# Softmax probabilities turned by VectorE and a way through DRAM instead of TensorE turns

## The chip, the cores and the metric

The kernel runs on one core of a Trainium2 chip. The metric is the device time of one execution in microseconds (us): the median of three runs. The core has five engines with queues of their own. TensorE (PE) multiplies matrices, VectorE (DVE) and GpSimd (POOL) do elementwise work and reductions, ScalarE (ACT) does exponentials and copies, and SyncE (SP) issues transfers. Sixteen DMA engines move data between on-chip memory (SBUF) and DRAM. Matmuls write to PSUM, eight banks of on-chip memory.

## The reference, cut to what matters

A two-layer decoder works on 16 blocks of 128 tokens with 512 features. Six parts follow each other, each added to x and normalized:

```python
x = _layernorm(x + _L0_attn_ref(x, ...))            # stage 1: softmax attention, 16 heads of 32, 4 key heads
x = _layernorm(x + _L0_xattn_ref(x, ctx_512, ...))  # stage 2: latent attention, 16 heads, keys = values = ctx rows
x = _layernorm(x + _L0_ffn_ref(x, ...))             # stage 3: ternary FFN
x = _layernorm(x + _L1_attn_ref(x, ...))            # stage 4: linear attention with decay
x = _layernorm(x + _L1_xattn_ref(x, ctx_512, ...))  # stage 5: causal softmax attention, 16 heads of 32
x = _layernorm(x + _L1_ffn_ref(x, ...))             # stage 6: mixture of experts
```

The softmax attentions, stages 1, 2 and 5, all have this form, for each block and head:

```python
scores = q @ k.T            # 128 queries x 128 keys
p = softmax(scores + mask)
out = p @ v                 # then projected and added to x
```

TensorE sums over the partitions (rows) of its operands. The softmax leaves p with the queries on the partitions; the product with the values needs the keys there. So each 128 x 128 square of p has to be turned.

## The kernel before

All of x stays in SBUF. Each stage is written as Python loops that a planner unrolls: it places each instruction in its engine's queue by the times of its own model, so the order on an engine is mostly not the order of the source. `tc.keep_in_program_order` pins an instruction behind the one traced before it on the same engine. On the chip each engine's queue then runs strictly in that order, SP's too.

Stages 1 and 5 share `attend`. Step n of its loop writes the scores of block n into four PSUM banks (`score`, L446 in stage 1 and L939 in stage 5). It then goes through four parts c. In each part the class `Softmax` starts one quarter of the block's heads (mask sum L184 and maximum L186 on VectorE, four exponentials L191 on ScalarE), finishes an earlier quarter (reciprocal L197 on VectorE, product L198 on POOL), and turns a quarter of block n - 1 (`turn`: four transposes L203 on TensorE into a PSUM bank, one copy L205 back by VectorE). At the top of the step the values of block n - 2 are multiplied (`value`, L452 and L946), copied by ScalarE (L246), and in part 1 projected, added to x and normalized (`project_out`, L148, L149, L110 to L121). The other parts are filled by `Share.deal` with tasks that prepare the next group of four blocks: transposes of x, projections, and in stage 1 the folding of stage 2's weights (`folds`), whose 1.7 MB pieces SP loads into two buffers (L391). In stage 5's last group there are no tasks left; in stage 1's last group only folds.

Stage 2 works in 32 steps: four groups, two halves of eight heads, four blocks each. Step m computes scores (`Heads`, L576), the softmax, and in `turn` lets VectorE transpose p in squares of 32 x 32 (L590) without moving the squares between rows. Four heads go through one such instruction. The values (L600) make up for that: sixteen products, each with 32 rows of keys and 256 columns, four in different row quarters of the array, with a copy of the keys (`rep`) in the matching order. The `rep` copies are loaded from a DRAM buffer, `dkv`, to which the rotated context is written first (L383, L538). Step m's order in the source is: scores and softmax of m, first half of the projection of m - 2 (`out(0)`, L613), values of m - 1, second half of the projection of m - 2 (`out(1)`), then `pieces`, which loads two 352 KB pieces of FFN weights on SP (L466) and reduces or cuts earlier ones on VectorE.

Stage 5's start also fills 20 MB of DRAM with zeros for stage 6 (L899), and stage 6's copies of x to DRAM (`sums<-x`, L987) are issued by SP while stage 5 still runs.

Of the kernel before, what the change touches and what calls it, by code (L numbers as in the profile page):

```python
# [12 lines left out]
F32 = mybir.dt.float32  # L13
# [5 lines left out]
P = 128  # L19
NB = 16  # L20
D = 512
# [24 lines left out]
def decoder_kernel(ctx: ExitStack, tc: tile.TileContext, a: dict, out: bass.AP):  # L46
# [22 lines left out]

    psum = Banks()  # L70
# [4 lines left out]
    psum.share(mm=2, sc=4, pt=2)  # L75
# [98 lines left out]
    class Softmax:  # L174
# [5 lines left out]
        def start(self):  # L180
            src = self.sc
            if self.mask is not None:
                src = self.pool.tile([P, 4, P], F32, tag="t", name="t", bufs=3)
                nc.vector.tensor_tensor(src, self.sc, bc(self.mask, 4), ALU.add)  # L184
# [3 lines left out]
            if self.p is None:  # L188
                self.p = self.pool.tile([P, 4, P], F32, tag="p", name="p", bufs=5)
# [10 lines left out]
        def turn(self):  # L200
            pt = bank("pt", [P, 4, P], "pt")
            for j in range(4):
                nc.tensor.transpose(pt[:, j, :], self.p[:, j, :], ident)  # L203
            self.pT = self.pool.tile([P, 4, P], F32, tag="pT", name="pT", bufs=4)
            nc.vector.tensor_copy(self.pT, pt)  # L205
# [21 lines left out]
    def attend(pool, mask, wo, prepare, score, value):  # L227


        held = {}  # L230
# [3 lines left out]
        for n in range(NB + 2):  # L234
# [7 lines left out]
            if n >= 2:  # L242
                av = bank("pt", [P, KC, P], "av")
                value(av, n - 2, [s.pT for s in held.pop(n - 2)])
                oT = pool.tile([P, KC, P], F32, tag="oT", name="oT")
                nc.scalar.copy(oT, av)  # L246
            for c in range(4):
# [5 lines left out]
                if 1 <= n <= NB:  # L253
                    held[n - 1][c].turn()
                if c == 1 and n >= 2:
                    project_out(oT, wo, n - 2)
                else:
                    share.deal()
# [52 lines left out]
    with tc.tile_pool(name="p1", bufs=1) as p1:  # L311
# [52 lines left out]
        dkv = dram.tile([NB, P, DC], F32, tag="dkv", name="dkv")  # L364
# [8 lines left out]
        def rotate(g, ct, kvr, t2):  # L373
# [4 lines left out]
            def turn():  # L378
# [4 lines left out]
                nc.sync.dma_start(dkv[blocks].rearrange("b l d -> l b d"), kvr)  # L383
# [64 lines left out]
        def value(av, n, pT):  # L448
            v = groups[n // GB][1]
            for c in range(KV):  # L450
                rows = slice(c * HD, (c + 1) * HD)
                nc.tensor.matmul(av[rows], lhsT=v[:, n % GB, rows], rhs=pT[c], start=True, stop=True)  # L452
# [52 lines left out]
    with tc.tile_pool(name="p2", bufs=1, reuse_waits="tile") as p2:  # L505
        psum.share(mm=2, sc=2, av=4)
# [19 lines left out]

        Q = P // 4
# [3 lines left out]
        def context(g, kvr):  # L533
            reps = []
            for i in range(GB):
                rep = p2.tile([P, 4, DC], F32, tag="rep", name="rep", bufs=GB + 1)
                for qi in range(4):
                    nc.sync.dma_start(  # L538
                        rep[qi * Q : (qi + 1) * Q], dkv[g * GB + i].rearrange("(kj k) d -> k kj d", k=Q)
                    )  # L540
                reps.append(rep)
# [8 lines left out]
            return xT, kvT, reps  # L550
# [17 lines left out]
        class Heads:  # L568
            def __init__(self, b, half, qT, kT, rep):
                self.b, self.half, self.rep = b, half, rep  # L570
# [9 lines left out]
                self.turned = p2.tile([P, 8, 4, Q], F32, tag="pT", name="pT", bufs=2)  # L580
# [5 lines left out]
            def turn(self):  # L586
                p = self.p
                for par, s in enumerate(self.soft):
                    s.finish()
                    nc.vector.transpose(  # L590
                        self.turned[:, 4 * par : 4 * par + 4].rearrange("p h k q -> p (h k q)"),
                        p[:, par].rearrange("p h k -> p (h k)"),
                    )

            def values(self):
                av = [bank("av", [P, 8, Q], "av") for _ in range(4)]
                for kj in range(4):
                    for qi in range(4):
                        rows = slice(qi * Q, (qi + 1) * Q)
                        nc.tensor.matmul(  # L600
                            av[qi], lhsT=self.rep[rows, kj, :], rhs=self.turned[rows, :, kj, :],
# [826 lines left out]
```

## Time and profile before

| what | value |
|---|---|
| median of 3 runs | 2106.39 us (2104.89 to 2107.31) |
| the profiled execution | 2109.23 us, span 2107.5 us |
| PE, DVE, ACT, POOL busy | 97%, 41%, 30%, 31% of the span |
| mean granted TensorE clock | 0.995 |
| stage 1, first to last scores | 34.1 to 234.3 us |
| stage 2, first scores to last values | 283.9 to about 753 us |
| stage 5, first to last scores | 1314.2 to 1497.8 us |

A row of the profile's groups reads: line, engine, operation, output<-input, shapes, count, then busy time in us and the mean length of one in ns, then the idle time of the engine just before and what ended it. A row of the timeline reads: start, length, engine, line, operation, count. Float32 matmuls appear as two instructions each. An instruction's length includes its way through the pipeline, so neighbours overlap; what one costs its engine is seen from start to start. [...]

### The profile page before, as it was taken

What the parts mean: (1) busy time and instruction counts of PE and PEld (TensorE: products, weight loads), DVE (VectorE), ACT (ScalarE), POOL (GpSimd) and SP (SyncE); (2) the same over time, 40 slices, a digit from 0 to 9 for tenths busy, and PEclk for the clock granted to TensorE, in tenths of its full rate; (3) what the DMA queues carried; (4) which work ended last, traced back from release to release, by engine and by line L of the source; (5) the groups of instructions that cost most, each with busy time, mean ns of one, the idle gap of its engine ahead of it and who ended that gap; (6) DMA issues with size and microseconds to landing.
All of it is one profiled execution on the core that took longest, in us unless ns stands there. A gap on an engine that the chain in (4) does not pass through costs nothing. (4 is left out here: it accounts for less than half of the span.)

```text
span 2107.5 us, 26857 instructions
## 1 busy us (share of the span) xinstructions
PE 2053.2 (97%) x10117; PEld 1148.5 (54%) x10117; DVE 853.9 (41%) x1728; ACT 626.0 (30%) x2167; POOL 648.2 (31%) x674
## 2 busy tenths in 40 slices
PE   8999999999999999999999999999899999999997
PEld 5555554445454458888555444555544455555552
DVE  4667733444554243222123313777731122222224
ACT  3655533323333222222211112766622200000002
POOL 5565521211122122223223113455603222222223
PEclk9999999999999999999999999999999999999999
DMA  6011320212220010001300008600004279999974
GB/s 230 1 35 45 112 79 24 62 43 74 60 66 6 1 54 2 1 1 39 115 1 1 1 6 258 232 21 21 27 25 147 93 244 284 303 294 293 289 229 166
DMA packets 105362, 209.99 MB, mean 100 GB/s; under 512 B 27280, under 2 KB 65552, under 8 KB 98576
## 3 DMA queue, kind: packets, MB, share of 16 engines
q1 hardware_dynamic: 90336, 101.40, 15.4%
q0 software_dynamic: 13792, 105.55, 15.2%
q8 instruction: 80, 1.31, 0.3%
q10 hardware_dynamic: 1104, 1.31, 0.2%
q14 instruction: 50, 0.41, 0.1%
HBM read 159.66 MB, written 48.57 MB: 99 GB/s over the span
## 5 line engine op out<-in xcount | busy, mean ns | idle before, releaser
L198 POOL TENSOR_TENSOR p<-p,rs 128x512 f32<-128x512 f32 x192 | 201.1, 1048 | 505.4 <-DVE rs L197 478.3
L613 PE MATMUL po<-mT,cc 128*128 128x512 f32 x512 | 236.0, 605 | 0.0
L191 ACT ACTIVATE p<-t,nmx 128x128 f32<-128x128 f32 x512 | 198.6, 390 | 34.5 <-POOL p L198 8.8
L613 PEld LDWEIGHTS po<-mT,cc 128*128 128x128 f32 x512 | 92.2, 189 | 107.2 <-issue 103.6
L191 ACT ACTIVATE p<-sc,nmx 128x128 f32<-128x128 f32 x256 | 90.2, 373 | 147.4 <-DVE nmx L186 142.1
L114 POOL TENSOR_SCALAR ve<-mv 128x1 f32<-128x1 f32 x80 | 18.1, 227 | 328.2 <-DVE mv L112 316.2
L559 PE MATMUL pq<-xT,wqr 128*128 128x512 f32 x256 | 117.5, 602 | 1.0 <-ACT xT L128 0.7
L1171 ACT ACTIVATE rsg<-rg 128x352 f32<-128x352 f32 x39 | 18.1, 464 | 336.0 <-PE rg L1166 336.0
L148 PE MATMUL po<-wo,oT 128*128 128x512 f32 x256 | 116.8, 599 | 0.4 <-ACT qkT L416 0.4
L1166 PE MATMUL rg<-ew,xsT 128*128 128x352 f32 x312 | 101.2, 466 | 14.5 <-DMA ew<-in_l1f_w_dram,which 12.7
L783 PE MATMUL pq<-xT,wq 128*128 128x512 f32 x256 | 110.9, 594 | 1.0 <-ACT xT L128 0.7
L1187 PE MATMUL ry<-ew,ractT 128*128 128x512 f32 (+1 forms) x234 | 106.9, 592 | 0.0
L121 POOL TENSOR_SCALAR x<-x,mv,rstd 128x512 f32<-128x512 f32 x48 | 100.6, 2097 | 4.5
L1166 PE MATMUL ru<-ew,xsT 128*128 128x352 f32 x312 | 98.7, 459 | 0.0
L191 ACT ACTIVATION_READ_ACCUMULATOR p<-t,nmx 128x1 f32 x512 | 96.4, 188 | 0.0
L706 POOL TENSOR_TENSOR hl<-ht,hh 128x512 fp32r<-128x512 f32 x44 | 60.5, 1375 | 114.8 <-ACT hh L704 114.8
L1137 POOL DMA_INDIRECT ew<-in_l1f_w_dram,which x39 | 38.1, 976 | 185.9 <-PE ry L1187 163.3
L1197 POOL DMA_INDIRECT sums<-ry,place x39 | 62.0, 1590 | 105.7 <-DMA sums<-ry,place 66.4
L205 DVE COPY pT<-pt 128x512 f32<-128x512 f32 x128 | 86.5, 678 | 18.1 <-PE pt L203 18.1
L203 PEld LDWEIGHTS pt<-ident,p 128*128 128x128 f32 x512 | 59.8, 141 | 53.8 <-issue 44.6
L1049 PE MATMUL pg<-xT,sw_gu 128*128 128x512 f32 x192 | 86.5, 593 | 0.0
L1173 DVE TENSOR_TENSOR ract<-rsg,ru 128x352 f32<-128x352 f32 x39 | 20.3, 521 | 158.5 <-issue 145.5
(231 smaller groups left out, 3715.4 us busy)
## 6 DMA issues: line engine op xcount, KB each, us to landing
piece<-in_l0f_w_dram SPq DMA_DIRECT2D x48, 352.0 KB
raw<-in_l0x_raw_dram SPq DMA_DIRECT2D x8, 1728.0 KB
slots_x<-zero SPq DMA_DIRECT2D x1, 10023.0 KB
sums<-zero SPq DMA_DIRECT2D x1, 9984.0 KB
xs<-slots_x SPq DMA_DIRECT2D x156, 64.0 KB
rep<-dkv SPq DMA_DIRECT2D x64, 64.0 KB
sums<-x SPq DMA_DIRECT2D x16, 256.0 KB
sum<-sums SPq DMA_DIRECT2D x16, 256.0 KB
```

The lines of the kernel that those rows point to most:

```text
L121: engine.tensor_scalar(x[b], x[b], mean, rstd, ALU.subtract, ALU.mult)
L148: nc.tensor.matmul(po, lhsT=oT[:, c, :], rhs=wo[:, c, :], start=(c == 0), stop=(c == KC - 1))
L191: nc.scalar.activation(self.p[:, j, :], src[:, j, :], AF.Exp, bias=nmx[:, j : j + 1], accum_out=self.sm[:, j : j + 1])
L198: nc.gpsimd.tensor_tensor(self.p, self.p, spread(rs, P), ALU.mult)
L205: nc.vector.tensor_copy(self.pT, pt)
L559: nc.tensor.matmul(pq, lhsT=wqr[:, k, cols], rhs=xT[:, k, :], start=(k == 0), stop=(k == KC - 1))
L613: nc.tensor.matmul(self.po, lhsT=self.cc[:, 4 * par + j, :], rhs=mT[h], start=(par == 0 and j == 0), stop=(par == 1 and j == 3),)
L783: nc.tensor.matmul(pq, lhsT=wq4[k // 2][:, k % 2, c * P : (c + 1) * P], rhs=xT[:, k, :], start=(k == 0), stop=(k == KC - 1))
L1049: nc.tensor.matmul(dst, lhsT=sw_gu[:, k, at : at + P], rhs=xTs[g][:, k, :], start=(k == 0), stop=(k == KC - 1),)
L1166: nc.tensor.matmul(dst, lhsT=self.xT[:, k, :], rhs=gu[:, k, off : off + FE], start=(k == 0), stop=(k == KC - 1),)
L1187: nc.tensor.matmul(po, lhsT=self.actT[:mw, m_, :], rhs=dn[:mw, m_, :], start=(m_ == 0), stop=(m_ == 2))
L1197: nc.gpsimd.indirect_dma_start(out=sums, out_offset=bass.IndirectOffsetOnAxis(ap=place, axis=0), in_=y, in_offset=None, compute_op=ALU.add,)
```

## The change

In stages 1 and 5, `Softmax.turn` goes. A class `Turn` takes its place, two parts behind the exponentials. For each quarter VectorE transposes the 32 x 32 squares of p from SBUF to SBUF. After two quarters (512 KB) SP writes them to a DRAM buffer; after four, SP reads the block back in four transfers, one for each set of 32 keys, so that each square arrives on its keys' rows. The values of block n - 2 are now taken up in part 1 of step n, one block after the last square, and the projection moves to part 2. The value products keep their number and shape, and each is pinned behind what precedes it on TensorE. The mask sum is written into p itself.

In stage 2 the squares go the same way, with one write of 512 KB and four reads of 128 KB a step. The values become two products over all 128 keys with 512 columns, in place of sixteen; `rep` and `dkv` go. The zeros for stage 6 are written in the second group of stage 3 instead of at the start of stage 5. PSUM banks are shared out anew.

```diff
-    psum.share(mm=2, sc=4, pt=2)
+    psum.share(mm=3, sc=4, pt=1)
...
-        def turn(self):
-            pt = bank("pt", [P, 4, P], "pt")
-            for j in range(4):
-                nc.tensor.transpose(pt[:, j, :], self.p[:, j, :], ident)
-            self.pT = self.pool.tile([P, 4, P], F32, tag="pT", name="pT", bufs=4)
-            nc.vector.tensor_copy(self.pT, pt)
+    class Turn:
+        def __init__(self, pool):
+            self.pool = pool
+            self.away = dram.tile([P, 4, 2, 8 * Q], F32, tag="away", name="away", bufs=2)
+
+        def squares(self, c, p):
+            if c % 2 == 0:
+                self.sq = self.pool.tile([P, 4, 8, Q], F32, tag="sq", name="sq", bufs=2)
+            at = slice(c % 2 * 4, c % 2 * 4 + 4)
+            nc.vector.transpose(
+                self.sq[:, :, at, :].rearrange("p k h q -> p h k q"), p.rearrange("p h (k a) -> p h k a", a=Q)
+            )
+            if c % 2:
+                nc.sync.dma_start(self.away[:, :, c // 2, :], self.sq.rearrange("p k h q -> p k (h q)"))
+            if c == 3:
+                self.back()
+
+        def back(self):
+            self.pT = self.pool.tile([P, 4, 16, Q], F32, tag="pT", name="pT", bufs=1)
+            rows = self.away.rearrange("(t a) k n f -> k a t (n f)", a=Q)
+            for k in range(4):
+                nc.sync.dma_start(self.pT[k * Q : (k + 1) * Q].rearrange("a t h q -> a t (h q)"), rows[k])
...
-                if 1 <= n <= NB:
-                    held[n - 1][c].turn()
                 if c == 1 and n >= 2:
+                    av = bank("pt", [P, KC, P], "av")
+                    held.pop(n - 2)
+                    value(av, n - 2, turns.pop(n - 2).pT)
+                    oT = pool.tile([P, KC, P], F32, tag="oT", name="oT")
+                    nc.scalar.copy(oT, av)
+                of, part = divmod(4 * n + c - 2, 4)
+                if 0 <= of < NB:
+                    if part == 0:
+                        turns[of] = Turn(pool)
+                    turns[of].squares(part, held[of][part].p)
+                if c == 2 and n >= 2:
                     project_out(oT, wo, n - 2)
...
-        psum.share(mm=2, sc=2, av=4)
+        psum.share(mm=2, sc=4, av=2)
...
             def turn(self):
-                p = self.p
+                sq = p2.tile([P, 4, 8, Q], F32, tag="sq", name="sq", bufs=2)
+                away = dram.tile([P, 4, 8 * Q], F32, tag="away2", name="away2", bufs=2)
+                self.pT = p2.tile([P, 4, 8, Q], F32, tag="pT", name="pT", bufs=2)
                 for par, s in enumerate(self.soft):
                     s.finish()
                     nc.vector.transpose(
-                        self.turned[:, 4 * par : 4 * par + 4].rearrange("p h k q -> p (h k q)"),
-                        p[:, par].rearrange("p h k -> p (h k)"),
+                        sq[:, :, 4 * par : 4 * par + 4, :].rearrange("p k h q -> p h k q"),
+                        self.p[:, par].rearrange("p h (k a) -> p h k a", a=Q),
                     )
+                nc.sync.dma_start(away, sq.rearrange("p k h q -> p k (h q)"))
+                rows = away.rearrange("(t a) k f -> k a t f", a=Q)
+                for k in range(4):
+                    nc.sync.dma_start(self.pT[k * Q : (k + 1) * Q].rearrange("a t h q -> a t (h q)"), rows[k])
...
-                av = [bank("av", [P, 8, Q], "av") for _ in range(4)]
-                for kj in range(4):
-                    for qi in range(4):
-                        rows = slice(qi * Q, (qi + 1) * Q)
-                        nc.tensor.matmul(
-                            av[qi], lhsT=self.rep[rows, kj, :], rhs=self.turned[rows, :, kj, :],
-                            start=(kj == 0), stop=(kj == 3),
-                        )
+                for par in range(2):
+                    av = bank("av", [P, 4, P], "av")
+                    tc.keep_in_program_order(nc.tensor.matmul(
+                        av, lhsT=self.keys,
+                        rhs=self.pT[:, :, 4 * par : 4 * par + 4, :].rearrange("p t h q -> p h t q"),
+                        start=True, stop=True,
+                    ))
+                    nc.scalar.copy(self.cc[:, 4 * par : 4 * par + 4, :], av)
```

## The prediction

> **What bounds the kernel now.** I read the page's busy table and slices first, then busy time in stretches that I chose by stage, then the order of time inside one block.
>
> ```profile
> span 2107.5 us, 26857 instructions
> PE 2053.2 (97%) x10117; PEld 1148.5 (54%) x10117; DVE 853.9 (41%) x1728; ACT 626.0 (30%) x2167; POOL 648.2 (31%) x674
> ```
>
> TensorE has no slack on average, so taking work from it should pay, unless another limit lies close behind. The stretches show where it does:
>
> ```profile
> 58.93:116.20 57.27, 56.59 (x388) 31.93 (x388) 39.88 (x82) 34.19 (x145) 33.13 (x33) 1.00 0.01 1
> 200.94:233.40 32.46, 32.21 (x258) 19.54 (x257) 28.51 (x60) 23.14 (x103) 18.24 (x18) 1.00 0.32 113
> 1336.94:1471.19 134.25, 132.92 (x1035) 75.28 (x1034) 98.12 (x199) 86.08 (x361) 69.05 (x70) 1.00 0.14 47
> 1479.20:1496.94 17.74, 16.81 (x177) 10.79 (x177) 17.32 (x38) 13.69 (x66) 13.67 (x14) 1.00 0.09 32
> ```
>
> Columns: stretch, length, busy PE, PEld, DVE, ACT, POOL, clock, DMA share, GB/s. Rows one and three are stages 1 and 5 with filler tasks: a block takes 14.2 and 13.4 us, VectorE is busy 9.8 of it: PE-bound. Row two, stage 1's last group, has 10.8 us a block and 9.5 of VectorE. Row four, stage 5's last group without filler, is VectorE's already: 17.32 of 17.74 us, two blocks, 8.9 each.
>
> **Stages 1 and 5: what goes.** 512 turns on PE and their 128 PSUM copies.
>
> ```profile
> L205 DVE COPY pT<-pt 128x512 f32<-128x512 f32 x128 | 86.5, 678 | 18.1 <-PE pt L203 18.1
> L203 PE MATMUL pt<-ident,p 128*128 128x128 f32 x512 | 79.2, 278 | 1.7 <-DVE pT L205 1.2 <-POOL p L198 0.5
> L590 DVE STREAM_TRANSPOSE pT<-p 128x512 f32<-128x512 f32 x64 | 45.5, 711 | 74.7 <-POOL p L198 74.7
> L1155 DVE STREAM_TRANSPOSE xsT<-xs 128x512 f32<-128x512 f32 x39 | 27.1, 698 | 0.0
> ...
> 1410.59 0.60 PE L203 MATMUL pt<-ident,p 128*128 128x128 f32 x4
> 1411.03 0.59 PE L137 MATMUL pq<-xT,wqo 128*128 128x512 f32 x1
> ```
>
> A turn lasts 278 ns, but four of them hold the next matmul back by 1411.03 - 1410.59 = 0.44 us: 0.11 us each. [...] I take the pitch, since it is what the following matmul sees: 16 x 0.11 = 1.75 us a block.
>
> In the filled part some 11 blocks of each stage turn before the last group: 11 x 1.75 = 19 us from each. Stage 1's last group stops at VectorE, about 9.8 instead of 10.8 us: 4 us. Stage 5's last group gains nothing.
>
> What takes their place on VectorE: the 128 copies at 678 ns become 128 square transposes, 698 to 711 ns by the two rows (L1155 is strided too): +0.03 us each, 4 us in all, hidden by 2.5 us of free VectorE in a filled block and on the path only in the last groups (0.5 us each). A strided transpose at half speed would add 0.7 x 4 = 2.8 us a block and fill VectorE; with a strided row at 698 I take nothing. The squares follow two parts behind the exponentials instead of four, so VectorE may wait for POOL when a layernorm (0.23 + 0.57 + 2.10 us) stands before the product; behind that wait stand the next mask sum and maximum. It eats VectorE's free time in filled blocks and costs up to 1 us a block in the last groups: +2 us in stage 5, in stage 1 inside the 9.8. The value products keep number and shape; their moving operand now comes in runs of 32 elements, as L600's does already (256 columns four at a time in 1.94/8 = 0.24 us, against half of 0.43 for 512): nothing. The mask sum in place saves a buffer, no time.
>
> **The way through DRAM.** A block issues on SP two writes of 512 KB and four reads of 256 KB; a stage 2 step one write of 512 KB and four reads of 128 KB. That is 192 + 160 new DMAs for 64 rep reads and 4 dkv writes removed. The nearest rows:
>
> ```profile
> 505.41 0.38 SPq L383 DMA_DIRECT2D dkv<-kvr  x1
> 506.00:506.50 0.50, 0.50 (x4) 0.20 (x4) 0.26 (x1) 0.50 (x2) 0.21 (x1) 1.00 0.28 83
> 506.50:507.00 0.50, 0.41 (x3) 0.30 (x2) 0.50 (x2) 0.14 (x1) 0.00 (x0) 1.00 1.04 291
> ...
> 488.45 1.75 SPq L538 DMA_DIRECT2D rep<-dkv  x4
> 490.00:490.50 0.50, 0.50 (x3) 0.19 (x2) 0.43 (x1) 0.00 (x0) 0.00 (x0) 1.00 0.44 129
> 490.50:491.00 0.50, 0.50 (x3) 0.26 (x2) 0.00 (x0) 0.00 (x0) 0.00 (x0) 1.00 0.56 149
> ```
>
> The write to DRAM starts 0.7 us after its issue and reaches 291 GB/s: 512 KB takes 1.8 us. The four 32-partition reads take 1.75 us to issue, begin to flow about 0.95 us after the first, and use half of the engines at 129 to 149 GB/s: about 280 at full use, so 512 KB takes 1.9 us and 1 MB 3.7. [...] Estimates: write 3.6 us, reads 4.0 in stage 2 and 5.8 in stages 1 and 5. [...]
>
> Stages 1 and 5: the values follow one whole block behind the last square, some 12.4 and 11.7 us in filled blocks: covered. The tails are not. In stage 5 the last scores start at 1496.94, the last multiplication ends at 1509.8, the last x sum starts at 1522.09. Now: square done 1510.6, + 9.4 trip, + 1.1 values, + 0.75 copy, + 3.7 projection = 1525.5: +3 us. Stage 1's tail likewise, +2, as stage 2's first projections can lie beside it. SP waits about 3.6 us in each block for a write; behind it stand raw, context, piece and sums DMAs, all issued a step or more ahead, so nothing. The reverse is worse: a raw load that waits for its fold (107 us at the longest today, harmlessly) can hold an away DMA. Between 0 and 12 us; I take +2. The 20 MB of zeros move to the FFN, where DMA stands at 0.00 to 0.01; matmuls there cannot mind (592 ns beside full DMA in stage 6, 594 without). Stage 5's start loses its collision: -1 of 1.7 us of idle PE.
>
> **Stage 2.**
>
> ```profile
> 481.59 1.16 PE L576 MATMUL sc<-kT,qT 64*128 64x128 f32 x16
> 482.68 3.70 PE L613 MATMUL po<-mT,cc 128*128 128x512 f32 x8
> 486.31 2.01 PE L600 MATMUL av<-pT,rep 32*128 32x256 f32 x32
> 488.25 3.70 PE L613 MATMUL po<-mT,cc 128*128 128x512 f32 x8
> ...
> 489.72 0.71 DVE L590 STREAM_TRANSPOSE pT<-p 128x512 f32<-128x512 f32 x1 [1.15 <-POOL p L198]
> ```
>
> Starts give 1.09 + 3.63 + 1.94 + 3.63 = 10.3 us a step. The values become 4 instructions of 0.43 us, and the change of row tiling before them (3.63 against 8 x 0.43) goes: 1.09 + 3.44 + 1.72 + 3.63 = 9.9, saving 0.41 x 32 = 13 us. The catch: transposes end 8.85 us after the step's scores, and in source order the values are due 9.9 + 4.7 = 14.6 after them. A trip of 5.7 us fits; 7.6 does not. If PE takes the second half of the projection (3.4 us, ready) before the values, 9.2 us fit. Only the values are pinned behind what precedes them, nothing behind them, and today's order already breaks L600 up by readiness. I count on that order, with +3 us of remaining stalls. Each half's first step has the 17 us projection as cover.
>
> **Sum.** -19 - 19 - 4 + 2 (tail) + 2 + 3 - 1 + 2 - 13 + 3 = -44 us. The profiled execution took 2109.2 us (span 2107.5): 2065; the median of the three runs is 2106.4, so 2062.
>
> That the change does not do what it says needs no rival: the turns are gone from the source, and only their order is open. **Rivals.** (a) Slower: stage 2's trip is not covered. In source order the step becomes 8.85 + trip - 4.7 us; 24 steps stand without a projection. The other terms bring -34, so it decides from 10.3 + 34/24 = 11.7 us a step, a trip of 7.6. [...] For: my estimate is on the edge. Against: the free order. (b) VectorE becomes the limit in filled blocks too, by waits for POOL or slow strided transposes: 0.7 us a block left of 1.75, -44 + 22 = 2084. Against: 2.5 us of free VectorE, L1155. (c) The order stays partly bad, or away DMAs stand behind waiting loads: 0.75 us on each of 56 value waits (16 + 24 + 16), -44 + 42: no difference, 2104. (d) The turns are worth their union of 79 us: 2045.
>
> **Chances.** Forecast 0.52, (d) 0.10, (b) 0.12, (c) 0.08, (a) 0.18. Three runs differ by 0.1%, so about 0.2% (4 us) can be told from no change. Faster 0.74, same 0.06, slower 0.20. Range 2036 to 2116: below, (d) with no tails (2045 - 9); above, (b), (c) and the edge of (a), whose rest is left out.
>
> **What would show it.** Right: L203 and L205 gone; about 12.4 and 11.7 us between score groups of filled blocks, stage 5's last group still about 9; stage 2 steps of 9.9; PE waits on the pT reads only in tails. Wrong: PE idle before stage 2's values for a DMA on each step; square transposes over 1 us; SP waits on L391 before away.

## The result, and the profile after

The changed kernel takes 2184.2 us (median of 4 runs, 2180.8 to 2184.8), the kernel before 2106.9 us: a ratio of 1.037 (95% interval 1.035 to 1.039). It is slower by 77 us, where 44 us less were forecast.

The page of the changed kernel says first that TensorE is as busy as before (2052.3 us for 2053.2), with 1408 instructions fewer:

```profile
span 2178.7 us, 24328 instructions
PE 2052.3 (94%) x8709; PEld 1122.9 (52%) x8709; DVE 852.0 (39%) x1728; ACT 623.7 (29%) x2103; POOL 647.4 (30%) x674
```

Busy time in stretches shows why. These are four blocks of stage 1's filled part, two of its last group, four filled blocks of stage 5 and five in its last group and tail (columns: stretch, length, busy PE, PEld, DVE, ACT, POOL, clock, DMA share, GB/s):

```profile
102.90:160.80 57.90, 54.15 (x319) 29.87 (x319) 38.06 (x80) 34.33 (x147) 32.44 (x32) 1.00 0.65 177
214.70:260.50 45.80, 28.15 (x130) 16.91 (x129) 20.68 (x47) 18.64 (x85) 17.79 (x18) 0.71 0.68 204
1396.80:1465.70 68.90, 61.96 (x353) 34.48 (x352) 39.28 (x80) 33.79 (x144) 27.88 (x28) 0.82 0.50 138
1538.00:1593.00 55.00, 36.25 (x241) 18.52 (x240) 27.97 (x59) 19.82 (x91) 25.37 (x25) 0.81 0.70 187
```

A filled block of stage 1 takes 14.5 us (14.3 before) and one of stage 5 17.2 (13.4 before), with idle TensorE that was not there. In the last groups TensorE is idle for more than a third of the time, the others about half of it or more. The granted clock is at 0.71 and 0.81 there, and at 0.82 in the filled blocks of stage 5, where it was 1.00. The slow clock stretches what work is left, by 47 us more than before (table below), which is why the busy time did not fall.

By stage, in the profiled runs: stage 1 (first scores to stage 2's first) 249.8 to 282.1 us, stage 2 (to the first product of stage 3) 484.7 to 483.7, stage 5 (first scores to the end of the last projection) 207.8 to 254.1. For stages 1 and 5 I add up, over windows of 2 us, TensorE's idle time and the busy time lost to the clock (busy x (1 - granted clock)). What remains of the length is work at full clock:

| kernel | stages 1 + 5 | idle | lost to the clock | work |
|---|---|---|---|---|
| before | 457.6 | 10.8 | 3.4 | 443.4 |
| changed | 536.2 | 77.9 | 50.6 | 407.7 |
| e2 without the trip | 457.8 | 43.9 | 17.3 | 396.6 |
| e7 without the trip, reordered | 439.8 | 33.2 | 19.1 | 387.5 |
| e8 rearranged, whole trip | 503.4 | 67.8 | 28.2 | 407.4 |
| e17 turns only left out | 431.9 | 21.3 | 12.6 | 398.0 |

TensorE did lose 36 us of work; 67 us of pauses and 47 us of slower clock came in its place. The waits on TensorE of the changed kernel (for what, us in all, times, longest):

```profile
PE po L149 <- ACT oT L273: 32.1, 30, 2.7
PE av L474 <- DMA pT<-away: 12.5, 2, 9.8
PE av L965 <- DMA pT<-away: 11.4, 3, 5.4
...
PE sc L958 <- DVE p L187: 9.5, 10, 3.7
PE sc L468 <- DVE p L187: 8.5, 5, 2.7
```

Only 24 us of these are waits for the trip's data. The rest are the projection behind ScalarE's copy of the values, and scores for banks that VectorE's mask sum has not yet freed. The first belongs to the copy's new place: of the kernels below it is 25.5 us in e2, and 3.3 in e6, where the copy is back in its old one. The second shows wherever the turns are gone, in e17 too, where nothing took their place (9.8 us ahead of scores, 0.5 before). One place on TensorE's timeline shows how a pause is paid twice:

```profile
1392.30 4.53 PE L958 MATMUL sc<-kT,qT 32*128 32x128 f32 x24 [3.71 <-DVE p L187]
1396.76 1.94 PE L965 MATMUL av<-pT,v 128*32 128x128 f32 x32
1399.40 6.50 PE L149 MATMUL po<-wqo,oT 128*128 128x512 f32 x8 [0.70 <-ACT oT L273]
...
1414.70 5.40 PE L149 MATMUL po<-wqo,oT 128*128 128x512 f32 x8 [2.69 <-ACT oT L273]
```

After 3.71 us of waiting, the same eight projection instructions that take 3.6 us elsewhere take 6.50: from 1391.4 to 1405.1 the granted clock is 0.50.

SP's queue in stage 1's last group shows what the trip's reads stand behind:

```profile
219.61 0.31 SPq L225 DMA_DIRECT2D pT<-away  x1
224.89 0.36 SPq L413 DMA_DIRECT2D raw<-in_l0x_raw_dram  x1
225.29 1.76 SPq L225 DMA_DIRECT2D pT<-away  x3
...
250.06 0.35 SPq L413 DMA_DIRECT2D raw<-in_l0x_raw_dram  x1
250.46 0.43 SPq L225 DMA_DIRECT2D pT<-away  x1
```

One read of four is out at 219.6; the other three wait 5.3 us for a fold to free a raw buffer, and then run behind 1.7 MB. The values that need the read of 250.46 come at 260.48, after 9.81 us of idle TensorE, the longest pause of these stages. In stage 5 the place of the raw load is taken by the copy of x for stage 6:

```profile
1542.16 2.87 SPq L217 DMA_DIRECT2D away<-sq  x2
1553.84 0.34 SPq L1006 DMA_DIRECT2D sums<-x  x1
1554.42 1.76 SPq L225 DMA_DIRECT2D pT<-away  x4
1556.23 1.20 SPq L217 DMA_DIRECT2D away<-sq  x2
```

From 1480 us on, the reads of all nine blocks follow a `sums<-x`, which waits for the layernorm of an earlier block (SP's waits in 1480 to 1600: 75.3 us in 10 times for POOL's x). Five of the nine start 0.57 or 0.58 us behind it, so they were held by it alone; the other four then wait for the values of the block before (10.3 us). Layernorm, copy of x, read, values, projection and layernorm form a chain through SP. In the rows above a block's last write goes out at 1542.16 and its reads at 1554.42, 12.3 us later. That is the rule: over the 32 blocks of stages 1 and 5 the median is 12.1 us; in each stage's first block, with nothing ahead of the reads, it is 3.3.

Stage 2 has the forecast step:

```profile
447.17 1.16 PE L589 MATMUL sc<-kT,qT 64*128 64x128 f32 x16
448.26 6.28 PE L631 MATMUL po<-mT,cc 128*128 128x512 f32 x14
454.37 1.88 PE L619 MATMUL av<-pT,kvr 128*128 128x512 f32 x4
456.09 1.02 PE L631 MATMUL po<-mT,cc 128*128 128x512 f32 x2
...
457.15 1.16 PE L589 MATMUL sc<-kT,qT 64*128 64x128 f32 x16
```

9.98 us from scores to scores (9.9 forecast, 10.3 before), and the second half of the projection does stand ahead of the values. Yet the stage is 1 us shorter, not 10.

### The profile page after: what moved, and what is told of

It reads as the page before. It is cut to its first block, busy times and chain, and to the rows that moved or that the text cites. A ratio compares the mean times of both kernels' runs of the same rounds, so it can differ in the third digit from the quotient of the medians.

```text
span 2178.7 us, 24328 instructions
## 1 busy us (share of the span) xinstructions
PE 2052.3 (94%) x8709; PEld 1122.9 (52%) x8709; DVE 852.0 (39%) x1728; ACT 623.7 (29%) x2103; POOL 647.4 (30%) x674
## 4 chain that ended last, share of the span: by engine, by line
PE 74%; DMA 9%; DVE 5%; ACT 4%; issue 4%; POOL 3%; SPq 0%; ACTq 0%; POOLq 0%; DVEq 0%
PE po L631 9%; PE po L149 8%; PE pq L572 5%; PE pq L813 5%; DMA ew<-in_l1f_w_dram,which 4%; PE pq L138 4%; PE pa L725 4%; PE pb L725 4%; PE po L752 4%; PE ry L1206 3%; PE rg L1185 3%; PE ru L1185 3%; PE po L138 3%; PE pv L821 3%; DMA slots_x<-row,slot 2%
## 5 line engine op out<-in xcount | busy, mean ns | idle before, releaser
L192 ACT ACTIVATE p<-p,nmx 128x128 f32<-128x128 f32 x512 | 198.6, 391 | 105.7 <-DVE nmx L189 75.4
L631 PEld LDWEIGHTS po<-mT,cc 128*128 128x128 f32 x512 | 95.4, 191 | 117.4 <-issue 107.5
L149 PE MATMUL po<-wo,oT 128*128 128x512 f32 x256 | 126.3, 640 | 15.4 <-ACT oT L273 15.4
L213 DVE STREAM_TRANSPOSE sq<-p 128x512 f32<-128x512 f32 x128 | 86.8, 693 | 31.9 <-POOL p L199 18.6
L192 ACT ACTIVATION_READ_ACCUMULATOR p<-p,nmx 128x1 f32 x512 | 96.9, 189 | 0.0
L149 PE MATMUL po<-wqo,oT 128*128 128x512 f32 x128 | 78.9, 773 | 16.8 <-ACT oT L273 16.7
L149 PEld LDWEIGHTS po<-wo,oT 128*128 128x128 f32 x256 | 49.0, 202 | 85.8 <-issue 53.7
L1216 POOL DMA_INDIRECT sums<-ry,place x39 | 62.0, 1590 | 96.3 <-DMA sums<-ry,place 47.5
```

What stands on the lines that cost most here:

```text
L149: nc.tensor.matmul(po, lhsT=oT[:, c, :], rhs=wo[:, c, :], start=(c == 0), stop=(c == KC - 1))
L192: nc.scalar.activation(self.p[:, j, :], src[:, j, :], AF.Exp, bias=nmx[:, j : j + 1], accum_out=self.sm[:, j : j + 1])
L631: nc.tensor.matmul(self.po, lhsT=self.cc[:, 4 * par + j, :], rhs=mT[h], start=(par == 0 and j == 0), stop=(par == 1 and j == 3),)
```

## The experiments

Medians of 4 or more runs, against the kernel before on the same chip (2103.5 to 2107.1 us). An edit also makes the planner order the queues anew, so a difference between two kernels holds the edit and the new order; where that mattered it is said. The runs come in five groups (e1 to e4, e5 to e8, e9 to e12, e13 to e16, e17 and e18), on four chips. A difference across groups is less sure by some us, since the kernel before itself differs by up to 3.6 us between them.

**e1, stage 2 alone.** Stages 1 and 5 as before, the rest of the diff kept.

> Stages 1 and 5 as before the change, stage 2 (the cross attention) as after it. In the two traces the loss stands in stage 1 (+32 us to the first scores of stage 2) and stage 5 (+46 us), while stage 2 takes 504 us against 506. Theory: the parts do not act on each other, so this kernel is at the time before, 2106, give or take 4, and up to 6 below it if the pause at stage 2's start (about 9 us of idle TensorE) came from stage 1's late end. Rival: stage 2's own saving of 13 us is there and was eaten by the slow clock that stage 1's pauses leave behind: 2093. Other rival: the stages disturb each other through the scheduler's order, and stage 2 alone is slower, 2115 or more.

2105.8 us, ratio 1.000 (0.999 to 1.001). The change in stage 2 alone costs nothing and gains nothing; the whole loss comes with the change in stages 1 and 5.

**e2, no trip in stages 1 and 5.**

```diff
-            if c % 2:
-                nc.sync.dma_start(self.away[:, :, c // 2, :], self.sq.rearrange("p k h q -> p k (h q)"))
...
-            for k in range(4):
-                nc.sync.dma_start(self.pT[k * Q : (k + 1) * Q].rearrange("a t h q -> a t (h q)"), rows[k])
+            self.pT = fixed[id(self.pool)]
```

> Leaves out, in stages 1 and 5, the writes of the squares to DRAM and the reads back; the values multiply a constant tile in place of the turned probabilities. VectorE's squares, the banks and the order of the source stay. Theory: the trip (its length, the single buffer that it is read back into, and its place on SP's queue) is the whole of the loss, and the turns are then worth what was forecast, 19 + 19 + 4 us: 2106 - 42 = about 2064, with the granted clock near 1.0 in both stages. Rival: a good part of the loss is on the compute engines (the copy of the values straight ahead of the projection, 32 us of waits; score banks held by VectorE, 18 us): then only the late values at the ends of the stages go, some 31 + 40 us: about 2113, and the filled blocks stay at 13.9 and 13.5 us.

2099.8 us (0.9985, 0.9975 to 0.9994). Each theory holds in part. The trip is worth 84 us (81 by the ratios to the kernel before), but with it gone only 5 of the 42 us appear, and none of them in stages 1 and 5 (457.8 us for 457.6). TensorE's work there fell by 47 us, and 47 us came back as pauses and clock. VectorE's timeline has the new order:

```profile
53.80 0.14 DVE L198 RECIPROCAL rs<-sm 128x4 f32<-128x4 f32 x1
55.16 0.71 DVE L214 STREAM_TRANSPOSE sq<-p 128x512 f32<-128x512 f32 x1 [1.22 <-POOL p L199]
55.79 0.14 DVE L198 RECIPROCAL rs<-sm 128x4 f32<-128x4 f32 x1
57.15 0.71 DVE L214 STREAM_TRANSPOSE sq<-p 128x512 f32<-128x512 f32 x1 [1.22 <-POOL p L199]
```

Reciprocal, POOL's product and square of one quarter follow each other, 1.99 us each round with 1.22 of it idle, and the next block's mask sums stand behind. This order is e2's own: its squares wait 95.4 us in all, the changed kernel's 31.9.

**e3, two buffers for the read back**, with `bufs=2` on pT (and room made elsewhere).

> The read back goes into two buffers in turn instead of one (room comes from one probabilities tile less in stage 1 and a single xT in stage 5). SP then does not wait for the values of the block before (53.0 and 31.8 us of waits after the change). Theory: the single buffer makes a chain of read, values, read at the ends of both stages: with two, stage 5's last group and tail lose most of their +41 us and stage 1's some 15 us of its +31: about 2184 - 45 = 2139. Rival: the reads are late because they stand behind the raw loads and the writes on SP, or because the trip itself is too long; then less than 10 us goes: 2174 or more.

2178.3 us (1.035, 1.033 to 1.037): 6 us less by the medians, 4 by the ratios, whose intervals overlap, so hardly anything. The rival is right. SP's waits for the values of the block before are gone, and the reads are as late, since they stand behind other things: SP waits 77.3 us for the x of `sums<-x` in stage 5's last group and tail, as it did with one buffer (75.3).

**e4, that and no raw loads in the last group.**

> The kernel with two buffers, and four of the 1.7 MB raw loads of stage 1's last group left out (the folds there work on the first two raw tiles again, so the folded weights of eight heads are other ones). Theory: a raw load that waits on SP for its buffer holds the reads behind it, and then its own 1.7 MB go ahead of them: without the loads stage 1's last group loses what the second buffer left there, 15 us more than the kernel with two buffers: about 2124. Rival: the raw loads cost nothing that the buffer did not: the two kernels agree within 4 us.

2160.6 us (1.026, 1.024 to 1.029), 18 less than e3; stage 1 alone 279.8 to 266.0. The raw load ahead of the reads costs what the theory said, about 14 us in its stage.

**e5 to e7, the order without the trip.** e5 moves the squares from two parts to four behind the exponentials; e6 moves the values and their copy back ahead of the four parts; e7 does both. The first two lines are e5's and e7's, the rest, ahead of the four parts, e6's and e7's.

```diff
-                of, part = divmod(4 * n + c - 2, 4)
+                of, part = divmod(4 * n + c - 4, 4)
...
+            if n >= 2:
+                av = bank("pt", [P, KC, P], "av")
...
+                value(av, n - 2, turns.pop(n - 2).pT)
...
+                nc.scalar.copy(oT, av)
```

> The kernel without the trip in stages 1 and 5 (the values multiply a constant tile), with the squares put four parts behind the exponentials, as the turns were, instead of two. The kernel without the trip only came to 2099.8: its VectorE runs reciprocal and square of the same quarter in turn and waits 94.8 us for POOL's products between them. Theory: this wait on VectorE is what uses up the 42 us that TensorE no longer works; four parts behind, the product is long done, the wait goes below 20 us, and the time to about 2075. Rival: the copy of the values that stands on ScalarE behind two groups of exponentials is the cause; then 2095 or more, with the 25 us of waits for it still there.

> The kernel without the trip, with the values and their copy put back ahead of the block's four parts, as they were before the change, the squares left two parts behind. Theory of VectorE's wait: the copy no longer stands behind exponentials, its 25 us of waits go, but VectorE still waits for POOL, so 2090 or so. Rival (the copy's place is the cause): 2070, with the granted clock back at 0.99.

> The kernel without the trip, with both: squares four parts behind, values ahead of the parts. This is the forecast's ideal for stages 1 and 5: the turns gone, nothing in their place on the path. Forecast's terms: 19 + 19 + 4 less than before, 2106 - 42 = 2064. If the pitch of 0.11 us a turn overstates what TensorE gains, 2080 or more; if the union of 79 us is right, 2040 or less.

2092.5, 2103.6 and 2084.0 us (ratios 0.992, 0.989 to 0.995; 0.997, 0.996 to 0.999; 0.988, 0.985 to 0.991). Neither theory holds alone: e6's waits for the copy go (from 25.5 us to 3.3), but its scores wait more for mask sums (15.6 us for 7.4), and it gains nothing; both together give 16 us against e2. Nor is VectorE's wait for POOL what e5 gained by: it was to fall below 20 us and is still 78.3 (94.8 in e2, 80.0 in e7). By what later squares help is not shown. e7 is not the ideal of 2064: 22 us of the 42.

**e8, the whole trip, rearranged**: as e7, values three blocks behind, two buffers, each raw load issued when its buffer is free, and in each part the squares ahead of the next exponentials.

> With the whole trip again, so that it computes all of the attention: squares four parts behind, values three blocks behind the scores and ahead of the parts, two buffers for the read back, and each raw load issued when its buffer has just come free. Theory: the trip has a whole block of cover and nothing on SP holds it, so the filled blocks come to some 12.6 and 12.0 us; the tails get a bare trip (9 us each) and one more pass of the loop: 2064 + 20 = about 2085, faster than before. Rival: the writes and reads cost more than their cover (SP waits 3.6 us for each write, VectorE's next square waits for its buffer): 2115 or more.

2145.2 us (1.017, 1.013 to 1.020). Half of the loss is gone and half is not: 61 us over e7. The rival had the right number. Its signs are there only in part: squares wait 4.7 us for writes, and TensorE 18 us for the reads.

**e9, the trip issued but not waited for.**

```diff
-                    value(av, n - 2, turns.pop(n - 2).pT)
+                    turns.pop(n - 2)
+                    value(av, n - 2, fixed[id(pool)])
```

> All writes and reads of the trip are issued as in the changed kernel (one buffer for the read back), but in stages 1 and 5 the values multiply a constant tile, so nothing on TensorE waits for the trip (stage 1 has one probabilities tile less, to make room). Theory: the loss is the lateness of the values and what stands behind them, so this kernel is at the time of the one without the trip, 2100. Rival: it is what the trip does on the other queues (SP in order, VectorE's squares waiting for their buffers, DMA beside TensorE); then 2150 or more, with VectorE's squares waiting for the writes.

2178.4 us (1.036, 1.034 to 1.039): most of the theory falls. No value waits for the trip, and the time is that of the changed kernel.

By stage it is not quite the same: in the profiled run stages 1 and 5 take 518.4 us, 18 less than in the changed kernel and 61 more than in e2, and a single pause of 11.0 us stands at stage 2's start, where POOL rotates the next context ahead of the first product.

The rival had the number, but not its reasons. In stages 1 and 5 the computing engines wait for a transfer once, VectorE's square for 4.5 us, and beside the transfers the instructions are hardly slower (VectorE is busy 158.7 and 152.4 us in the two stages, 158.6 and 153.5 in e2; ScalarE 137.4 and 130.6 for 135.6 and 131.6). What is left is the order in which the planner put the queues; VectorE's leaves that of e2 at its 42nd instruction in stage 1 and its 45th in stage 5. This is reached by elimination; no run has the trip in e2's order.

In stage 5 the first ten starts of values lie as in e2 (119.2 us for 119.0); from there to the last start it takes 86.3 us for 59.6. There, TensorE and VectorE:

```profile
1532.97 1.12 PE L963 MATMUL sc<-kT,qT 32*128 32x128 f32 x8 [3.60 <-DVE p L187]
...
1540.19 6.09 PE L149 MATMUL po<-wqo,oT 128*128 128x512 f32 x8 [0.36 <-ACT oT L278]
1549.88 2.04 PE L963 MATMUL sc<-kT,qT 32*128 32x128 f32 x8 [3.60 <-DVE p L187]
```

```profile
1546.32 0.69 DVE L150 TENSOR_TENSOR x<-x,po 128x512 f32<-128x512 f32 x1 [4.42 <-PE po L149]
...
1547.87 1.29 DVE L215 STREAM_TRANSPOSE sq<-p 128x512 f32<-128x512 f32 x2
1549.08 0.65 DVE L187 TENSOR_TENSOR p<-sc,causal 128x512 f32<-128x512 f32 x1
```

A circle of 16.9 us: the sum into x waits for the projection, squares and mask sum stand behind it, scores wait for the mask sum, and the projection, which after that pause takes 6.09 us instead of 3.6, is late again.

**e10, e11, scores pinned** in the source's order, in the changed and in the rearranged kernel.

> The changed kernel with the score products of stages 1 and 5 kept in the order of the source (quarter by quarter in turn, as before), where the changed kernel's order takes them bank by bank as banks come free. In the traces the scores' busy time rose from 25.2 + 24.2 to 42.5 + 43.9 us. Theory: the products of one bank use the same quarter of TensorE's rows and follow each other, those of four banks lie beside each other; kept together they give back some 25 us or more: 2159 or less. Rival: they were apart only because their banks were still held, and together they wait for the last bank as long: 2180 to 2188.

> The rearranged kernel with the whole trip (2145.2) with its scores kept in the source's order too; there their busy time is 36.6 + 34.3 us. Theory (the broken scores cost their busy time): 2125. Rival (they wait for the last bank instead): 2142 to 2148.

2215.4 us (1.054, 1.051 to 1.056) and 2162.9 (1.028, 1.026 to 1.030): 31 and 18 us worse, beyond both theories. Kept together the scores do cost less: 18.8 us of busy time in each stage in e10, and TensorE's work in the two stages falls by 31 us. But its idle time there grows by 65 (77.9 to 142.7), and the waits for the copy of the values reach 95.1 us. That the scores wait for the last bank is the likely reason, not one that the waits show.

**e12, the gap filled** with two idle products.

> The changed kernel with two idle products of 128x512 more in each block of stages 1 and 5, between the values and the projection that waits for their copy (32 blocks, 27 us of added work, in place of 32.1 us of waits in 30 places; nothing reads their result). Theory: these waits pull the granted clock down, and the lower clock costs 19.0 + 31.6 us in the two stages; with the waits filled, the added work costs nothing, and the clock gives back half of that or more: 2184 - 25 = 2159. Rival: the clock falls for the longer pauses only (late reads, held banks); then the time stays, 2180 to 2195, and the clock in the windows with it.

2193.4 us (1.043, 1.040 to 1.046). I had the added work wrong: two products are four instructions, 1.75 us a block, 56 us in all. Of these 56 us the kernel shows 9. In the two stages idle time fell by 25 us and the clock's loss by 14.5 (50.6 to 36.1). So the pauses do pull the clock down; filling these gave back 14.5 us of the 25 or more expected.

**e13, e14, e16, the sum into x a block later**, in the changed kernel, the rearranged one, and the one without the trip. What `sums` holds is the sum into x and the layernorm.

```diff
-                if c == 2 and n >= 2:
-                    project_out(oT, wo, n - 2)
+                if c == 1 and sums:
+                    sums.pop(0)()
+                if c == 2 and n >= 2:
+                    sums.append(project_only(oT, wo, n - 2))
```

> The changed kernel, with the sum of the projection into x (and the layernorm behind it) issued a block later, behind two mask sums of the next block, instead of right after the projection. Theory of the circle (projection, sum into x, mask sums behind it on VectorE, score banks, scores, projection): VectorE no longer waits 38.1 + 44.7 us for projections, the banks come free sooner, the pauses and with them the lower clock shrink; 2184 - 35 = about 2150. Rival: VectorE's wait was slack and only moves to the reciprocals and the squares; 2178 to 2190.

> The rearranged kernel with the whole trip (2145.2) with the same later sum into x. Theory of the circle: 2145 - 20 = 2125. Rival (slack): 2140 to 2150.

> The kernel without the trip, with squares four parts behind and values ahead of the parts (2084.0), and the later sum into x. There VectorE seldom waits for a projection, so the circle hardly runs: 2080 to 2086. If the later sum helps here too by 15 us or more, it does something else than break the circle.

2183.4, 2145.6 and 2083.2 us: nothing in all three (ratios 1.037, 1.034 to 1.039; 1.020, 1.017 to 1.022; 0.989, 0.987 to 0.991), though e14's five runs lie 22 us apart (2129.2 to 2151.0), so that a small gain could hide there. The circle is seen in e9's trace, but it is not what holds the changed kernel. In stage 5 a later layernorm also makes `sums<-x`, and with it the read behind it on SP, later; the read of e13's values at 1564.80 is waited for 3.12 us.

**e15, the projection pinned behind the filler** as well.

> As the rearranged kernel with the later sum into x, and the projection also kept behind the filler products that the source puts ahead of it, so that the copy of the values lies beside them. In the rearranged kernel TensorE waits 10.2 + 18.7 us for that copy. If those waits count in full with the clock behind them, 30 us less than without the pin: about 2095, below the kernel before; if the filler is missing elsewhere instead, within 5 us of it.

2137.8 us (1.015, 1.012 to 1.018), 8 less than e14, not 30, and with e14's spread not clear of nothing. The waits for the copy hardly changed, in stage 5 (12.8 us for 12.5) as in stage 1 (9.7 for 9.8); why the filler did not cover them is not shown.

**e17, only the turns left out of the kernel before.**

> The kernel before the change, in which the turns on TensorE in stages 1 and 5 are left out: VectorE copies the probabilities as they are, so the values multiply untransposed ones. Nothing else is changed; no squares, no trip. By the forecast's pitch (0.11 us a turn) 42 us go: 2064. Theory after the runs: the turns filled pauses that the chain scores, mask, exponentials, product, values, projection leaves in each block, so that of 56 us of TensorE time most comes back as pauses and lower clock, as in the kernel without the trip: 2080 to 2090.

2075.7 us (0.986, 0.984 to 0.988): 30.5 us less. TensorE's work fell by 45 us (the pitch gives 56 for all 512 turns, and 42 of them were booked as time); 20 us of it came back, half as pauses, half as clock. By stage, stage 5 is 16.8 us shorter, where 19 were forecast, and stage 1 only 8.9, where 23 were. The windows around one pause of TensorE (2.27 us ahead of scores that wait for VectorE):

```profile
139.00:141.00 2.00, 2.00 (x26) 1.82 (x22) 2.00 (x3) 1.51 (x6) 1.25 (x2) 1.00 0.72 290
141.00:143.00 2.00, 0.19 (x2) 0.00 (x0) 2.00 (x4) 2.00 (x8) 1.42 (x2) 0.88 1.02 435
143.00:145.00 2.00, 1.55 (x6) 1.35 (x7) 2.00 (x6) 0.08 (x1) 1.13 (x1) 0.50 0.14 50
145.00:147.00 2.00, 2.00 (x5) 0.97 (x4) 0.82 (x2) 1.70 (x8) 1.26 (x1) 0.50 0.00 0
147.00:149.00 2.00, 2.00 (x3) 0.77 (x3) 1.62 (x4) 2.00 (x12) 1.17 (x2) 0.50 0.00 0
```

Busy at 0.50 from 143 to 149: (1.55 + 2.00 + 2.00) x 0.50 = 2.8 us lost on top of 2.3 us of pause.

**e18, stage 2 alone, its pauses filled.** e1's trace has the pause at the stage's start, where all late folds stand ahead of the first turn:

```profile
300.04 1.96 PE L593 MATMUL av<-pT,kvr 128*128 128x512 f32 x4 [1.58 <-DMA pT<-away]
305.73 7.63 PE L605 MATMUL po<-mT,cc 128*128 128x512 f32 x10 [3.74 <-ACT cc L598]
```

```diff
-                while late:
+                for _ in late[:4]:
                     late.pop(0)[1]()
-        psum.share(mm=2, sc=4, av=2)
+        psum.share(mm=4, sc=2, av=2)
```

> Stages 1 and 5 as before, stage 2 as changed (2105.8), with two edits: the late folds are spread over the first three steps, four tasks each, instead of all before the first turn, and the banks are shared as four for products and two for scores instead of two and four. In the trace stage 2 has 15.4 us of idle TensorE and 5.3 us of lower clock against 4.9 and 0.5 before. Theory: its step is 9.9 us as forecast and the gain of 13 us went into the pause at its start (5.6 us and 4 us of clock behind it) and at the group boundaries (1 to 2 us each); filled, 2106 - 12 = 2094, faster than before. Rival: the trip is on the edge in every step, and the folds only move the pause: 2102 to 2108.

2093.9 us (0.9937, 0.9923 to 0.9951): faster than the kernel before by 12 us and than the changed one by 90. Stage 2 takes 471.9 us, 12.8 less than before; idle time is 8.0 us for e1's 15.4, the clock's loss 0.3 for 5.3. The two edits were not separated. At the same place:

```profile
300.66 1.95 PE L593 MATMUL av<-pT,kvr 128*128 128x512 f32 x4 [0.18 <-issue]
303.64 7.13 PE L605 MATMUL po<-mT,cc 128*128 128x512 f32 x16 [1.03 <-ACT cc L598]
```

## Why the prediction was wrong, point by point

- **The turns, -42 us.** The pitch of 0.11 us was about right as TensorE's work (56 us for all turns; 45 in e17, 56 by the same count in e7). As time it was too much: 30.5 us in e17. (The first stretch gives a block of 57.27 / 4 = 14.3 us with VectorE busy for 10.0, not 14.2 and 9.8; nothing rests on it.) "PE-bound" was read from a busy share of 97%; the turns were also what TensorE did while copy, mask sum and product ran, and without them those links show.
- **The squares two parts behind, +2.** Too small: without the trip, four parts behind instead of two is worth 7 to 14 us (e5 against e2, on two chips, by medians or by ratios) and 20 us (e7 against e6). The wait that the step named, POOL ahead of the square, is there (94.8 us in e2), but it is not what the later squares took away (80.0 in e7), so the mechanism stays open.
- **The copy of the values** moved from the top of the step into part 1, behind two groups of exponentials on ScalarE. No term had it. With late squares its old place is worth 8.5 us (e7 against e5), with early ones nothing (e6 against e2).
- **The trip in stages 1 and 5: covered, +5 for tails, +2 for held transfers.** This is the step that failed: 84 us in place of 7 (changed against e2). The trip was counted from the last square on as a write of 3.6 us and reads of 5.8. The reads in fact go out 12.1 us after the last write (median), and with values that wait for them take 7.5 to 7.7 us more in stage 5's last blocks: some 20 us, against a cover of 12. Most of it passes on SP's queue before the reads are issued. The text looked for one transfer that holds a trip's, the raw load, and took it at 2 us; it costs about 14 in its stage (e4). The sums were looked at only as what a write may hold ("all issued a step or more ahead, so nothing"), but they stand ahead of every late read in stage 5. That they wait was to be seen before: SP waits 179.0 us in 16 times for their x in the kernel before (L987). And pT has one buffer, which the text did not see; that alone is 4 to 6 us, within the noise (e3). Waits for the trip's data are only 24 us of the loss: without any of them e9's stages 1 and 5 still take 61 us more than e2's, by elimination for the order in which the planner puts the queues.
- **The trip's own length.** In stage 2 it was right: a write lands 2.6 us after its issue and four reads 4.4 after the first one (medians in e14), 7.0 us for 7.6. No run shows by itself the 1.1 us that the write's 3.6 and the reads' 4.0 and 5.8 each hold beyond the rows (2.2 of the 9.4 us in the tail): the write's 0.7 and 1.8 us make 2.5 of the 2.6 alone. In stages 1 and 5 the reads were too short: 8.0 us in e14 for 5.8. The text reckoned on 280 GB/s at full use of the engines, from 129 to 149 at half; with the engines full, at shares of 1.07 and 1.05, the changed kernel's last reads reach 229 and 221 (1588 to 1590 us).
- **Clock.** The sum counted at full clock. 47 us of the loss in the changed kernel is busy time at a lower one.
- **Stage 2, -13 and +3 of stalls.** The step of 9.9 us and the order ahead of the values were right, the trip was covered, and rival (a), on which most of the chance of slower lay, did not come about. TensorE's work fell by some 15 us, but pauses and clock, at the start and at group boundaries, grew by as much (20.7 us in e1, 5.4 before), where 3 were booked; they could be filled (e18).
- **Rival (c)**, an order that "stays partly bad" or away transfers behind waiting loads, had the mechanism, with a chance of 0.08 and at 42 us half of what the trip cost: it priced the waits, not the clock behind them.

**What stays open.** The trip's 81 to 84 us are shown as a sum. The raw loads (14) are shown by themselves; the rearrangement takes back 39 in all. That `sums<-x` holds the reads of stage 5, and that the chain through SP sets the pace of its last group, is read from the trace: no run took those copies away. How much of the rest is the trip and how much the order that the planner gives with the trip in it was not separated by a run: e9 points to the order, by elimination.

## What to carry to other kernels

A TensorE that is 97% busy may still hold filler: leave a piece out (as e17 does) before its time is booked as gain, and price the waits that come to light. Count what a new transfer stands behind on its queue, for each stage, with what each of those transfers waits for. A pause of TensorE can be paid twice, by its length and by the clock behind it (2.3 and 2.8 us at the place in e17); over stages 1 and 5 as a whole the clock added 0.4 to 0.65 of the idle time (17.3 to 43.9 us in e2, 50.6 to 77.9 in the changed kernel). Where a pause can be filled with work that is due anyway, as at stage 2's start, both come back (idle time 15.4 to 8.0 us, the clock's loss 5.3 to 0.3, from e1 to e18).

## What the runs showed of the hardware that I had not expected

In the trace of the changed kernel all seven pauses of TensorE of 2.6 us or more that began at full clock (2.67 to 9.81 us) were followed, before 2 us after their end, by a granted clock of 0.50. Of the twenty pauses of 1.3 to 2.4 us seven were and thirteen were not (2.05 us ahead of 227.72: 0.50 from 227.47 on; 2.37 us ahead of 218.18: 1.00 until 227.47), and in e17 one of 1.75 us was (ahead of 85.39: six windows of 1 us at 0.50). Of the thirty of 0.6 to 1.2 us four were.

The clock record of the changed kernel shows more. It has 19 stretches at 0.50 that end before the kernel does, and they last 3.41, 6.83, 10.24, 13.65 or 17.07 us; the two in the record of the kernel before last 6.83 us each. Ahead of them TensorE was not always idle: in the 3.41 us before each of the 19 it was busy for 0 to 47% of the time in twelve cases and for 64 to 96% in seven. In the last 3.41 us of each of the 19 it was busy for 83% or more. Counted back from 227.47 us in steps of 3.41 us, the pause of 2.37 us lies across two steps, which are busy for 1.99 and 2.46 us, and that of 2.05 us nearly all in one, which is busy for 1.60 us. That such a pause is followed by the slow clock or not by where it lies is my reading of these two places, not shown by a run. Full of work, 3.41 us at 0.50 cost 1.7 us (3.41 x 0.50).

A block's scores, taken over its four banks in turn, need 1.17 us for 32 instructions (at 1336.94 us in the kernel before). Broken up by banks, their busy time in stage 1 rose from 25.2 us to 42.5 in the changed kernel, a part of it at the lower clock; keeping them together brought it to 18.8 and cost more still in pauses (e10).
